# A state loop whose side work is handed out by whole uses of a PSUM bank, with delta's last piece in three and two buffers for the shared expert's copies

## The chip, the cores and the metric

One core of one Trainium2 chip runs the whole kernel in one launch. Five engines work from queues of their own and meet through semaphores: PE (TensorE, matmuls into PSUM; PEld are its weight loads), DVE (VectorE), ACT (ScalarE), POOL (GpSimd) and SP (SyncE, which issues most DMAs). The metric is device time in microseconds (us), the median of several runs.

## The reference, cut to what matters

Input x has 64 rows of 64 tokens with 256 features; `cond_1024` has one vector of 256 for each row. Four residual blocks follow. The change lies in the third (a selective state space layer, "mamba", after a recurrent layer) and in the shared expert of the fourth (a mixture of experts):

```python
x = x + L0_attn(L0_cond(x, cond))
x = x + L0_ffn(L0_cond2(x, cond))
x = x + L1_attn(L1_cond(x, cond))          # recurrent layer, then mamba
x = x + L1_ffn(L1_cond2(x, cond))          # mixture of experts, then SwiGLU experts

# L1_attn (mamba): d_inner 512, n 16
xi, z = split(x @ W_in)
xc = silu(conv4(xi) + b_conv)
delta_lr, B, C = split(xc @ W_xproj)
delta = softplus(delta_lr @ W_dt + b_dt)
dA = exp(delta[..., None] * A)
dBx = delta[..., None] * B[:, :, None, :] * xc[..., None]
h = dA_t * h + dBx_t;  y = einsum(h, C_t) + D * x_t      # scan over time
out = (y * silu(z)) @ W_out

# L1_cond2: shared experts beside eight routed ones (top 2)
for e in range(2):
    h = silu(x @ s_w1[e].T) * (x @ s_w3[e].T)
    shared_out += h @ s_w2[e].T
```

## The kernel before

**Chunks and steps.** `mamba` cuts the 4096 tokens into eight chunks of 512 (`NCH`, `CH`). With features on partitions, d_inner makes four tiles of 128 (`NI`), taken in pairs (`PI` = 2), and n is 16 states (`S`). One step of the state loop handles one pair and one state: 2 x 16 = 32 steps (`STEPS`) to a chunk and 256 in all.

**What a step does.** DVE runs two scans over time (L1094, one for each tile of the pair) in place in `hb` and multiplies both by C, broadcast over the partitions as `cb` (L1096). PE transposes the product with an identity matmul into PSUM, where the 16 states are summed (`yp`, L1109: eight matmuls). For later steps, POOL makes dx times B (`hb`, L1046, two steps ahead in the program), SP fetches B from DRAM spread over the partitions (`Bn`, L993), ACT makes dA = exp(delta * A) for the next step (L1053, two of them), and PE makes the next `cb` by a matmul with one column picked (L998). `dA` lies in PSUM in three buffers, `cb` in one, `hb` in SBUF in five.

**Side work.** Beside the steps, generators yield the rest in small pieces, from three sources:
- `urgent`: `finish` (transposes y back, L1006; adds D * x on DVE, L1008; multiplies by the gate on POOL, L1009), and after a chunk's last step `project` (the output matmuls, L1023, and the residual's add on DVE, L1026).
- `pieces`: of the next chunk, `head` (input matmuls L919 and the convolution on DVE, L926; Silu L930; the matmul L934 for delta, B and C; delta by pairs, L950 to L973), and of this chunk, `gates` (matmuls L982, copies L985, Silu L988).
- `others`: of the chunk before, `Mixture.beside`: router scores (L1499), choosing and sending rows to the experts (`send`), and the shared expert (`shared`: matmuls L1820, copies L1824 and L1827, Silu L1831, POOL's product L1828, the second matmul L1836 and its copy L1840).

A piece that leaves a sum open in PSUM yields `MID`. All of `urgent` and `pieces` use one PSUM bank, `mp`, with one buffer; all of `others` use one bank, `mq`. `turn` (L1072) hands out a piece of `urgent`, or of `pieces` where `urgent` has none; after a `MID` from either it asks `pieces`. The loop calls `turn` so that `LEFT` = 40 pieces are handed out in a chunk: 31 of `pieces` and nine of `urgent`. `islice` at j = 0 lets the head run up to the end of the first pair's delta before the second pair's gates. `BESIDE` = 56 pieces of `others` are handed out in a chunk beside that (`BESIDE_LAST` = 72 in the last).

**Delta.** Softplus is put together from functions: Relu and Abs (L959, L960), Exp (L962), two Identities (L963, L964), a subtraction (L967), Ln (L969), then an add, a subtraction and the product with xc (L970 to L972). The last four were one piece. The arithmetic is on DVE in the first chunk and on POOL in the others.

**Shared expert.** `shared` works through a chunk in two halves of 256 tokens. In each half four results of the matmul with `s3` and the rows of the output pass through an SBUF tile "up", of which the pool `work` has one buffer. `send` keeps its input in a tile "xr" of the same pool.

**What sets the order.** A scheduler takes the program's order as priority and, with estimates of its own of when things are ready, fixes each engine's queue; each engine then works its queue in order. `tc.stamp_issue_order_token` holds scans and multiplies in the program's order.

Of the kernel before, what the change touches and what calls it, by code (L numbers as in the profile page):

```python
# [13 lines left out]
F32 = mybir.dt.float32  # L14
# [7 lines left out]
P = 128  # L22
B, L, D = 64, 64, 256
NT = B * L
CH = 512
NCH = NT // CH
KD = D // P
# [830 lines left out]
MID, END = "mid", "end"  # L858


def mamba(g, w, hs, beside):
# [3 lines left out]
    nc, tc = g.nc, g.tc  # L865
    NI, S, R = w.NI, w.S, w.R
# [3 lines left out]
    NB = 2  # L870
    PI = 2
    STEPS = NI // PI * S
    LEFT = 40
    BESIDE = 56
    BESIDE_LAST = 72
    hs2 = hs.rearrange("p k b t -> p k (b t)")
# [1 line left out]
    with (  # L878
# [17 lines left out]
        rows = 2 * 32 + S  # L896
# [12 lines left out]
        def head(c, v):  # L909

            tok = ts(c, CH)
            v.xc = p2.tile([P, NI, CH], F32, name="xc")
            v.delta, v.dx, v.sz, v.ready = [], [], [], 0
            v.dbc = p1.tile([W, CH], F32, name="dbc")
            v.parts = parts[c % 2]
            for i in range(NI):
                ps = one()
                for k in range(KD):
                    nc.tensor.matmul(ps, w.Win[:, k, ts(i, P)], hs2[:, k, tok], start=(k == 0), stop=(k == KD - 1))  # L919
                    if k == 0:  # L920
                        yield MID
                acc = v.xc[:, i, :]
                nc.scalar.activation(acc, ps, AF.Identity, bias=w.col[:, 0, i : i + 1], scale=w.taps[:, i, 3:4])
                for s in range(1, 4):
                    to = seq(acc)[:, :, s:]
                    nc.vector.scalar_tensor_tensor(  # L926
                        to, seq(ps)[:, :, : L - s], w.taps[:, i, 3 - s : 4 - s], to, ALU.mult, ALU.add
                    )
                yield
            nc.scalar.activation(v.xc, v.xc, AF.Silu)  # L930
            yield
            ps = one()
            for i in range(NI):
                nc.tensor.matmul(ps[:W, :], w.Wxp[:, i, :], v.xc[:, i, :], start=(i == 0), stop=(i == NI - 1))  # L934
                if i < NI - 1:
                    yield MID
            nc.scalar.copy(v.dbc, ps[:W, :])

            v.B = tc.dram_tile((S, CH), F32, name=f"B{c}")
            nc.sync.dma_start(v.B, v.dbc[R : R + S, :])  # L940


            r = slice(C0, W)
            nc.scalar.copy(v.parts[32 : 32 + S, :], ps[r, :])
            nc.vector.tensor_sub(ps[r, :], ps[r, :], v.parts[32 : 32 + S, :])
            nc.scalar.copy(v.parts[0:S, :], ps[r, :])
            nc.vector.tensor_sub(v.parts[64 : 64 + S, :], ps[r, :], v.parts[0:S, :])
            yield


            for i0 in range(0, NI, PI):
                z, u = (p3.tile([P, PI, CH], F32, name=n) for n in ("delta", "dx"))
                v.delta.append(z)
                v.dx.append(u)
                t2, t3 = (p1.tile([P, PI, CH], F32, name=n) for n in ("t2", "t3"))
                for i in range(PI):
                    ps = one()
                    nc.tensor.matmul(ps, w.Wdt[:, ts(i0 + i, P)], v.dbc[:R, :], start=True, stop=True)
                    nc.scalar.activation(z[:, i, :], ps, AF.Relu, bias=w.col[:, 1, i0 + i : i0 + i + 1])  # L959
                    nc.scalar.activation(u[:, i, :], ps, AF.Abs, bias=w.col[:, 1, i0 + i : i0 + i + 1])  # L960
                    yield
                nc.scalar.activation(u, u, AF.Exp, scale=-1.0)  # L962
                nc.scalar.activation(t2, u, AF.Identity, bias=unit[:, 0:1])  # L963
                nc.scalar.activation(t3, t2, AF.Identity, bias=unit[:, 1:2])  # L964
                yield
                e = nc.gpsimd if c else nc.vector
                e.tensor_sub(u, t3, u)  # L967
                yield
                nc.scalar.activation(t2, t2, AF.Ln)  # L969
                e.tensor_add(z, z, t2)  # L970
                e.tensor_sub(z, z, u)
                e.tensor_mul(u, z, v.xc[:, i0 : i0 + PI, :])  # L972
                v.ready += PI  # L973
                yield
# [94 lines left out]
        urgent, pieces, others = iter(()), iter(()), iter(())  # L1069
        mid = None  # L1070

        def turn():  # L1072

            nonlocal mid
            got = next(pieces, None) if mid else next(urgent, END)
            if got is END:
                got = next(pieces, None)
            mid = got

        for s in range(LAST):  # L1080
            c, j = divmod(s, STEPS)
            p, n = divmod(j, S)
            now = vs[c]
            if j == 0:
                ahead = head(c + 1, vs[c + 1]) if c + 1 < NCH else iter(())
                pieces = chain(pieces, gates(c, now, 0), islice(ahead, 3 * NI + PI + 4), gates(c, now, PI), ahead)
                left = 0
            if n == 0:
                yp = [pp.tile([P, CH // P, P], F32, name=f"yp{i}") for i in range(PI)]
            hb, dA = hbs.pop(s), decays.pop(s)  # L1090

            for i in range(PI):
                h = hb[:, i, :]
                ins = nc.vector.tensor_tensor_scan(h, dA[i].rearrange("p b l -> p (b l)"), h, 0.0, ALU.mult, ALU.add)  # L1094
                tc.stamp_issue_order_token(ins.ins, "state")
            ins = nc.vector.tensor_tensor(hb, hb, cb.unsqueeze(1).to_broadcast([P, PI, CH]), ALU.mult)  # L1096
            tc.stamp_issue_order_token(ins.ins, "state")
            if s + AHEAD < LAST:
                ca, ja = divmod(s + AHEAD, STEPS)
                while vs[ca].ready <= ja // S * PI:  # L1100
                    turn()
                inputs(s + AHEAD)
            if s + 1 < LAST:
                decay(s + 1)
                cb = spread_c(vs[(s + 1) // STEPS], (s + 1) % S)

            for i in range(PI):
                for t in range(CH // P):
                    nc.tensor.matmul(  # L1109
                        yp[i][:, t, :],  # L1110
                        hb[:, i, ts(t, P)],
                        g.ident,
                        start=(n == 0 and t == 0),
                        stop=(n == S - 1 and t == CH // P - 1),
                        is_transpose=True,
                        skip_group_check=True,
                    )
            if n == S - 1:
                yT = [p1.tile([P, CH // P, P], F32, name=f"yT{i}") for i in range(PI)]
                for i in range(PI):  # L1120
                    nc.scalar.copy(yT[i], yp[i])
                urgent = chain(urgent, finish(c, now, p * PI, yT))
                if j == STEPS - 1:
                    urgent = chain(urgent, project(c, now))
            while left < (j + 1) * LEFT // STEPS:
                left += 1
                turn()
            most = BESIDE if c + 1 < NCH else BESIDE_LAST
            for _ in range((j + 1) * most // STEPS - j * most // STEPS):
                next(others, None)  # L1130
# [578 lines left out]
class Mixture:  # L1709
# [97 lines left out]
    def shared(self, c, x, work):  # L1807

        g, nc = self.g, self.g.nc
        NS = self.s1.shape[2] // P  # L1810
        UT = CH // 2
        for u in range(2):
            xu = x[:, :, ts(u, UT)]
            h = work.tile([P, NS, UT], F32, name="sh")
            for w in (self.s1, self.s3):
                for i in range(NS):
                    if i % 2 == 0:
                        ps = bank(g, (P, 2, UT))
                    for k in range(KD):
                        nc.tensor.matmul(ps[:, i % 2, :], w[:, k, ts(i, P)], xu[:, k, :], start=(k == 0), stop=(k == KD - 1))  # L1820
                    if i % 2:
                        to = h[:, i - 1 : i + 1, :]
                        if w is self.s1:
                            nc.scalar.copy(to, ps)  # L1824
                        else:
                            up = work.tile([P, 2, UT], F32, name="up")
                            nc.scalar.copy(up, ps)  # L1827
                            nc.gpsimd.tensor_mul(to, to, up)  # L1828
                    yield
                if w is self.s1:  # L1830
                    nc.scalar.activation(h, h, AF.Silu)  # L1831
                    yield
            ps = bank(g, (P, 2, D))
            for t in range(2):
                for i in range(NS):
                    nc.tensor.matmul(ps[:, t, :], h[:, i, ts(t, P)], self.s2[:, i, :], start=(i == 0), stop=(i == NS - 1))  # L1836
                    if i % 2 and (t, i) != (1, NS - 1):
                        yield
            rows = work.tile([P, 2, D], F32, name="up")
            nc.scalar.mul(rows, ps, 0.125)  # L1840
            to = self.made[c * CH + u * UT : c * CH + (u + 1) * UT, :]
            nc.sync.dma_start(to.rearrange("(t p) d -> p t d", p=P), rows)
# [346 lines left out]
```

## Time and profile before

The profile is of one execution. Its own time stands beside the runs':

| what | us |
|---|---|
| median of 3 runs | 2806.84 (2806.24 to 2814.49) |
| profiled execution | 2807.03 |
| its span, from the first to the last instruction | 2804.6 |
| DVE busy in the span | 1770.7 (63%) |
| PE busy | 2339.3 (83%) |
| ACT busy | 1375.5 (49%) |
| POOL busy | 1340.5 (48%) |
| first to last scan of the state loop | 698.5 to 1845.7 |

In the profile, a row of a group gives the line, the engine, the operation, what it writes and reads, the count, then busy time and mean length, and the engine's idle time before it with what ended it. "A <- B" in the waits means that A could start only when B had ended. A wait for several things is put down to the one that came last.

### The profile page before, as it was taken

The numbers are of one execution on the slowest core, as the hardware profiler recorded it, in microseconds if no ns is written. First come the engines' busy times: TensorE is split into PE (matmuls) and PEld (weight loads), VectorE is DVE, ScalarE is ACT, GpSimd is POOL, SyncE is SP. The second block draws the span as 40 slices with busy tenths as digits, with TensorE's granted clock in tenths as the row PEclk, the third lists the DMA queues.
The fourth block names the chain that finished last, engine by engine and source line by source line (L and its number), as shares of the span: only waits on it lengthen the run. The fifth ranks groups of instructions, "written<-read, shape, count | busy, mean of one in ns | idle before, by whom it ended". The sixth has DMA issues, their size and how long they took to land.

```text
span 2804.6 us, 34388 instructions
## 1 busy us (share of the span) xinstructions
PE 2339.3 (83%) x11977; PEld 1674.0 (60%) x11996; DVE 1770.7 (63%) x2980; ACT 1375.5 (49%) x2289; POOL 1340.5 (48%) x1166
## 2 busy tenths in 40 slices
PE   3989967996568888887978888687786989999995
PEld 3634436773345555554655555566664768888884
DVE  0477748973999898888889797852353442322333
ACT  0567528885466757584757676533232222222220
POOL 0022345521696868685878787835555331111110
PEclk9979988997769999998999999899998999999997
DMA  9999820002112122221121222325685755555655
GB/s 224 372 358 347 276 70 1 1 1 90 68 68 83 65 74 70 72 72 57 65 92 67 83 81 75 106 70 178 212 287 194 278 216 206 214 192 197 227 192 189
DMA packets 180501, 406.03 MB, mean 145 GB/s; under 512 B 24785, under 2 KB 84434, under 8 KB 174946
## 3 DMA queue, kind: packets, MB, share of 16 engines
q1 hardware_dynamic: 166882, 366.80, 38.4%
q0 software_dynamic: 13440, 36.98, 3.4%
q8 instruction: 96, 1.57, 0.2%
q14 instruction: 83, 0.68, 0.1%
HBM read 280.76 MB, written 144.98 MB: 152 GB/s over the span
## 4 chain that ended last, share of the span: by engine, by line
PE 43%; DVE 21%; ACT 13%; issue 9%; POOL 5%; another core or an unknown queue 2%; DMA 1%; DVEq 0%; SPq 0%; ACTq 0%; POOLq 0%
DVE hb L1094 12%; PE ps L1684 11%; PE acc L1582 8%; PE out L450 4%; DVE hb L1096 3%; ACT dA L1053 2%; PE ps L1651 2%; PE yp L1109 2%; PE mq L1820 1%; DVE xc L926 1%; PE s L416 1%; PE acc L441 1%; ACT L1053 1%; PE mp L982 1%
## 5 line engine op out<-in xcount | busy, mean ns | idle before, releaser
L1046 POOL TENSOR_TENSOR hb<-dx,Bn 128x1024 f32<-128x1024 f32 x256 | 606.4, 2377 | 269.0 <-PE yp L1109 219.7
L1094 DVE TENSOR_TENSOR_SCAN hb<-dA,hb 128x512 f32<-128x512 f32 x512 | 602.1, 1210 | 63.2 <-ACT dA L1053 59.8
L1053 ACT ACTIVATE dA<-delta,negA 128x504 f32<-128x504 f32 x512 | 345.6, 685 | 303.5 <-DVE hb L1094 298.3
L1109 PEld LDWEIGHTS yp<-ident,hb 128*128 128x128 f32 x2048 | 264.4, 150 | 160.2 <-issue 121.2
L1096 DVE TENSOR_TENSOR hb<-hb,cb 128x1024 f32<-128x1024 f32 x256 | 312.4, 1220 | 66.3 <-PE cb L998 48.0
L1684 PE MATMUL ps<-gxT,w 128*128 128x256 f32 (+1 forms) x1600 | 324.5, 361 | 1.2 <-DVE gxT L1559 0.8
L1684 PEld LDWEIGHTS ps<-gxT,w 128*128 128x128 f32 x1600 | 276.3, 190 | 47.2 <-issue 12.4
L1820 PE MATMUL mq<-x,moe_s 128*128 128x256 f32 x896 | 244.5, 405 | 66.1 <-ACT up L1827 29.9
L1109 PE MATMUL yp<-ident,hb 128*128 128x128 f32 x2048 | 298.6, 290 | 0.0
L1358 POOL DMA_INDIRECT ffn_y<-gy,to x72 | 69.2, 962 | 432.3 <-ACT gy L1584 419.8
L1820 PEld LDWEIGHTS mq<-x,moe_s 128*128 128x128 f32 x896 | 166.6, 200 | 131.7 <-ACT sh L1824 42.5
L1688 DVE TENSOR_TENSOR gh<-gs,ps 128x256 f32<-128x256 f32 (+1 forms) x200 | 78.6, 394 | 213.5 <-ACT gs L1687 206.2
L1582 PE MATMUL acc<-w,gh 128*128 128x256 f32 (+1 forms) x864 | 190.0, 390 | 0.0
L1584 ACT ACTIVATE gy<-acc,wt 128x256 f32<-128x256 f32 x152 | 67.4, 474 | 246.8 <-PE acc L1582 227.5
L1687 ACT ACTIVATE gs<-ps 128x256 f32<-128x256 f32 (+1 forms) x200 | 72.4, 364 | 235.4 <-PE ps L1684 219.3
L998 PE MATMUL cb<-parts,pick 80*128 80x512 bf16 x256 | 104.5, 408 | 88.2 <-DVE hb L1096 83.9
L1582 PEld LDWEIGHTS acc<-w,gh 128*128 128x128 f32 (+1 forms) x864 | 146.8, 191 | 30.4 <-issue 13.2
L432 POOL TENSOR_TENSOR E<-E,z 128x1024 f32<-128x1024 f32 x32 | 61.6, 1925 | 194.5 <-DVE z L431 118.0
L1358 POOL DMA_INDIRECT moe_y<-gy,to x80 | 78.0, 975 | 110.2 <-ACT gy L1584 91.3
L1582 PE MATMUL acc<-w,rh 128*128 128x256 f32 x320 | 88.5, 419 | 45.6 <-ACT rh L1653 40.3
L1572 DVE TENSOR_REDUCE wt<-pick 128x2 f32<-128x4 f32 (+1 forms) x88 | 13.6, 156 | 174.7 <-ACT gy L1584 164.0
L450 PE MATMUL out<-oT,hs 128*128 128x512 f32 x256 | 117.8, 604 | 1.5 <-ACT oT L443 1.5
(470 smaller groups left out, 4457.1 us busy)
## 6 DMA issues: line engine op xcount, KB each, us to landing
w<-ffn_w SPq DMA_DIRECT2D x40, 2176.0 KB
Bn<-B SPq DMA_DIRECT2D x128, 512.0 KB
moe_x<-fill SPq DMA_DIRECT2D x130, 260.0 KB
ffn_x<-fill SPq DMA_DIRECT2D x129, 260.0 KB
w<-moe_w SPq DMA_DIRECT2D x48, 512.0 KB
ffn_w<-in_ffn_W_dram SPq DMA_DIRECT2D x16, 640.0 KB
gx<-moe_x SPq DMA_DIRECT2D x32, 260.0 KB
gx<-ffn_x SPq DMA_DIRECT2D x32, 260.0 KB
```

The source lines that it names most:

```text
L450: nc.tensor.matmul(ps, M[:, o, ts(k, P)], v.o[:, o], start=(o == 0), stop=(o == H // 2 - 1))
L998: nc.tensor.matmul(t, pick[:, n : n + 1].to_broadcast([rows, P]), v.parts, start=True, stop=True)
L1046: nc.gpsimd.tensor_mul(hb, vs[c].dx[p], Bn[:, n % NB, :].unsqueeze(1).to_broadcast([P, PI, CH]))
L1053: nc.scalar.activation(decays[s][i][:, :, 1:], seq(vs[c].delta[p][:, i, :])[:, :, 1:], AF.Exp, scale=A[:, p * PI + i, n : n + 1],)
L1094: ins = nc.vector.tensor_tensor_scan(h, dA[i].rearrange("p b l -> p (b l)"), h, 0.0, ALU.mult, ALU.add)
L1096: ins = nc.vector.tensor_tensor(hb, hb, cb.unsqueeze(1).to_broadcast([P, PI, CH]), ALU.mult)
L1109: nc.tensor.matmul(yp[i][:, t, :], hb[:, i, ts(t, P)], g.ident, start=(n == 0 and t == 0), stop=(n == S - 1 and t == CH // P - 1), is_tran ...
L1358: i = self.g.nc.gpsimd.indirect_dma_start(out=self.y, out_offset=bass.IndirectOffsetOnAxis(ap=to, axis=0), in_=y, in_offset=None)
L1582: nc.tensor.matmul(po[s], h, w, start=(i == 0), stop=(i == n - 1))
L1684: nc.tensor.matmul(ps[:, j, :], v.w12[:, k, ts(j * (full + 1) + i, P)], v.xT[:, k, :], start=(k == 0), stop=(k == KD - 1))
L1688: nc.vector.tensor_mul(v.h[:, i, : v.rows], s, ps[:, 1, :])
L1820: nc.tensor.matmul(ps[:, i % 2, :], w[:, k, ts(i, P)], xu[:, k, :], start=(k == 0), stop=(k == KD - 1))
```

## The change

`turn` keeps the source from which it took a piece that ended in `MID` and asks the same source again until a piece ends without it; so the uses of `mp` are handed out whole. Delta's last piece is split into three: Ln, the add, and the other two. Each group so has two pieces more; `LEFT` becomes 44, and the `islice` one group longer by two. The choice of engine `e` moves up some lines. In `shared` the copies of a half and its rows go in turn to the tile "xr" (of which they use a part) and to "up", beginning with "xr".

```diff
@@ -870,7 +870,7 @@
     NB = 2
     PI = 2
     STEPS = NI // PI * S
-    LEFT = 40
+    LEFT = 44
     BESIDE = 56
     BESIDE_LAST = 72
     hs2 = hs.rearrange("p k b t -> p k (b t)")
@@ -959,15 +959,17 @@
                     nc.scalar.activation(z[:, i, :], ps, AF.Relu, bias=w.col[:, 1, i0 + i : i0 + i + 1])
                     nc.scalar.activation(u[:, i, :], ps, AF.Abs, bias=w.col[:, 1, i0 + i : i0 + i + 1])
                     yield
+                e = nc.gpsimd if c else nc.vector
                 nc.scalar.activation(u, u, AF.Exp, scale=-1.0)
                 nc.scalar.activation(t2, u, AF.Identity, bias=unit[:, 0:1])
                 nc.scalar.activation(t3, t2, AF.Identity, bias=unit[:, 1:2])
                 yield
-                e = nc.gpsimd if c else nc.vector
                 e.tensor_sub(u, t3, u)
                 yield
                 nc.scalar.activation(t2, t2, AF.Ln)
+                yield
                 e.tensor_add(z, z, t2)
+                yield
                 e.tensor_sub(z, z, u)
                 e.tensor_mul(u, z, v.xc[:, i0 : i0 + PI, :])
                 v.ready += PI
@@ -1072,10 +1074,14 @@
         def turn():
 
             nonlocal mid
-            got = next(pieces, None) if mid else next(urgent, END)
-            if got is END:
-                got = next(pieces, None)
-            mid = got
+            if mid is None:
+                mid = urgent
+            got = next(mid, END)
+            if got is END and mid is urgent:
+                mid = pieces
+                got = next(mid, END)
+            if got is not MID:
+                mid = None
 
         for s in range(LAST):
             c, j = divmod(s, STEPS)
@@ -1083,7 +1089,7 @@
             now = vs[c]
             if j == 0:
                 ahead = head(c + 1, vs[c + 1]) if c + 1 < NCH else iter(())
-                pieces = chain(pieces, gates(c, now, 0), islice(ahead, 3 * NI + PI + 4), gates(c, now, PI), ahead)
+                pieces = chain(pieces, gates(c, now, 0), islice(ahead, 3 * NI + PI + 6), gates(c, now, PI), ahead)
                 left = 0
             if n == 0:
                 yp = [pp.tile([P, CH // P, P], F32, name=f"yp{i}") for i in range(PI)]
@@ -1809,6 +1815,15 @@
         g, nc = self.g, self.g.nc
         NS = self.s1.shape[2] // P
         UT = CH // 2
+
+        def spare():
+
+            if next(names) == "up":
+                return work.tile([P, 2, UT], F32, name="up")
+            t = work.tile([P, KD, CH], F32, name="xr").rearrange("p k t -> p (k t)")
+            return t[:, : 2 * UT].rearrange("p (a t) -> p a t", a=2)
+
+        names = cycle(("xr", "up"))
         for u in range(2):
             xu = x[:, :, ts(u, UT)]
             h = work.tile([P, NS, UT], F32, name="sh")
@@ -1823,7 +1838,7 @@
                         if w is self.s1:
                             nc.scalar.copy(to, ps)
                         else:
-                            up = work.tile([P, 2, UT], F32, name="up")
+                            up = spare()
                             nc.scalar.copy(up, ps)
                             nc.gpsimd.tensor_mul(to, to, up)
                     yield
@@ -1836,7 +1851,7 @@
                     nc.tensor.matmul(ps[:, t, :], h[:, i, ts(t, P)], self.s2[:, i, :], start=(i == 0), stop=(i == NS - 1))
                     if i % 2 and (t, i) != (1, NS - 1):
                         yield
-            rows = work.tile([P, 2, D], F32, name="up")
+            rows = spare()
             nc.scalar.mul(rows, ps, 0.125)
             to = self.made[c * CH + u * UT : c * CH + (u + 1) * UT, :]
             nc.sync.dma_start(to.rearrange("(t p) d -> p t d", p=P), rows)
```

## The prediction

> **What bounds the kernel now.** I read the sums by stage first. The state loop with its lead-in is the middle row; the columns are length, busy time and count of PE, PEld, DVE, ACT and POOL, clock, DMA share and GB/s.
>
> ```profile
> 0.00:690.00 690.00, 563.20 (x3556) 354.09 (x3576) 412.26 (x603) 403.98 (x750) 201.01 (x408) 0.92 0.54 177
> 690.00:1866.00 1176.00, 945.09 (x4336) 634.76 (x4335) 1021.27 (x1005) 747.19 (x1015) 879.27 (x468) 0.91 0.21 72
> 1866.00:2804.60 938.60, 830.98 (x4089) 685.18 (x4087) 337.13 (x1372) 224.34 (x525) 260.26 (x290) 0.94 0.60 212
> ```
>
> DVE is the fullest engine there: 1021 of 1176 us. Each of 256 steps needs two scans and one multiply, 1.21 + 1.21 + 1.22 = 3.64 us, 932 us in all, and the change removes no DVE work. It can only shorten DVE's idle time. DVE's waits between 700 and 1846 us say for whom it idles (total, times, longest):
>
> ```profile
> DVE hb L1094 <- ACT dA L1053: 59.8, 38, 7.6
> DVE hb L1096 <- PE cb L998: 48.0, 34, 4.9
> DVE hb L1094 <- POOL hb L1046: 3.1, 1, 3.1
> DVE mp L945 <- ACT parts L944: 2.3, 1, 2.3
> ```
>
> So about 113 us can be won or added to. I call the chunks c0 to c7 and their 32 steps j0 to j31, counted by scans in the timeline. The largest wait for PE (4.85 us) is c3 j5; the timeline shows what PE did (start, length, engine, what, idle before):
>
> ```profile
> 1132.30 1.03 PE L1836 MATMUL mq<-moe_s,sh 128*128 128x256 f32 x4
> 1132.91 2.33 DVE L1094 TENSOR_TENSOR_SCAN hb<-dA,hb 128x512 f32<-128x512 f32 x2
> 1135.16 0.66 DVE L1026 TENSOR_TENSOR x<-x,mp 128x512 f32<-128x512 f32 x1
> 1135.87 2.99 PE L982 MATMUL mp<-hs,Win 128*128 128x512 f32 x4 [2.55 <-DVE x L1026]
> 1138.66 1.75 PE L1836 MATMUL mq<-moe_s,sh 128*128 128x256 f32 x4
> 1140.25 0.38 PE L998 MATMUL cb<-parts,pick 80*128 80x512 bf16 x1
> 1140.67 1.22 DVE L1096 TENSOR_TENSOR hb<-hb,cb 128x1024 f32<-128x1024 f32 x1 [4.85 <-PE cb L998]
> ```
>
> The gate matmul (L982) wants bank mp, which the projection's add (L1026) frees; that add stands on DVE behind two scans, and the broadcast cb that the multiply needs stands on PE behind L982 and four L1836. The old hand-out produces this: after MID from the projection, the next piece comes from the other stream, which wants the same bank.
>
> **Whole uses of a bank.** The changed order (both programs' queues were compared) finishes the projection's two uses before any gate matmul. In c1 to c4 the second add then has a multiply between it and the next cb: one L984 of 1.1 us and two scores of 1.0 us fit, by the rows, into the 3.6 us until cb is wanted. So the waits of this kind in c2, c3 and c4 go: 4.85 + 4.85 + 3.16 = **-12.9 us**. In c5, c6 and c7 they do not. There the new queue at j3 reads projection x2, shared x2, projection x2, shared x2, cb, and the second pair, the start of the second use, waits for the first use's add, which is again queued behind the next step's scans. That is the shape of the 3.16 us row of c5 today; c5, c6 and c7 lose 3.16, 4.1 and 4.0 us now and get about 3.2 each: 0 to -2, taken as **-1**.
>
> New on PE: the four L934 matmuls no longer stand in three steps but together. 4 x 1.28 us (x4 records took 2.54) after the step's transposes, plus 1.04 for these and 0.4 for cb, overrun the 6.1 us between one multiply's end and the next-but-one's start by 1.3 in c1 to c3. At j6 and j8 a shared matmul waits for copies that ACT makes behind dA (and at j8 behind a table load and a Silu): 0.5 and 1.2 over by the same sum. 3 chunks x 3.0 = 9.0, against 2 x (0.83 + 1.1) of small waits in c2 and c3 that leave: **+5**. Small waits of this sort can't all be read from a queue; today about 16 of the 48 us are of them. I add **+5**; ends -3 and +16, should a second set arise.
>
> **Delta's last piece as three, LEFT 44, islice +6.** No arithmetic is added; 16 groups get two more yields, and 35 instead of 31 pieces (44 with the urgent 9) are given out per chunk. What moves is ACT's order. A step gives ACT 3.64 us, its two dA take 1.37, and with three dA buffers dA of step s may begin only when step s-2's last scan ended. So more than about 5 us between two dA makes DVE wait. Today c2 j30 has load 1.28, Silu 1.06, copy 0.58, delta 0.68, Silu 1.91, dx 0.68, copy 0.58, load 1.28 = 8.1 us there; adding up in queue order gives a wait of 3.3, and the trace has 3.0. The next burst (Ln between two loads and a copy, 4.2 us, at j0) gives 2.4; the trace has 2.36. In the changed order Ln stands at j31 without a wait, but Silu of shared (with loads 4.5 us) at j27 meets two copies, load, Silu, delta, dx, copy, load = 6.7 us at j28: a wait of 4.9. Added over all steps, c1 to c7, such bursts make 66 us today and 60 then. Today's 66 is really 54 (59.8 less one DMA wait of 5.8, below), so I scale by 0.8: **-5**. Per chunk: c1 +0.6, c2 and c3 -1.3 each, c4 -2.3, c5 +3.1, c6 +1.1, c7 -4.8, where the shared Silu leaves j0.
>
> Here a rule speaks against the change. The Trainium skill, "ScalarE: Activation LUTs", section "Table sets: the hidden batching unit", says to batch activations by table set and not to go back and forth. ACT's queue holds 92 table loads in the loop before and 104 after, because Silu, Ln and Exp are mixed more finely. By this trace's row (1283 ns each) the 12 are 15.4 us of ACT time; by the page's price of about 2.66 us for a switch, load plus drain, 32 us. In the trace dA starts 10 ns after its load ends, so the row decides. ACT is 64% busy here, so I charge only loads that lie in a burst; they are in the 60.
>
> POOL: the add and the subtract now follow at separate turns, its work stays 4 x 2.36 us a group, and POOL runs two to three steps ahead. Its one wait of 3.1 us (c1 j30): **-2**, ends 0 and -3. In chunk 7 the rows of a second send waited 6.7 us for the first's indirect writes and DVE 5.8 us for ACT behind it. In the new queue the eight writes start some four steps earlier and DVE's table work (about 14 us) covers the second eight: **-4**. If that cover fails, eight writes at 1.27 us (0.96 and 0.3 between) before hb make POOL late by 5: ends -5 and +3.
>
> **Two buffers for the shared expert.** What ACT waits for here is little: POOL's L1828 held "up" for 3.2 us in the whole loop, ACT's idle time, not DVE's. Directly it is worth 0. But the copies can be queued earlier, which shows at the loop's end:
>
> ```profile
> 1857.13 0.86 PE mq L1820 x4
> 1857.99 3.62 PE mp L1023 x8
> 1861.61 6.92 PE mq L1836 x32
> 1868.61 0.61 ACT up L1840
> ```
>
> These 32 records are 16 matmuls, 0.43 us each. Behind the last transposes PE has 24 shared matmuls before and 12 after: 12 x 0.43 = 5.2, and a 1.9 us Silu with its load falls before the last scan: **-6**, ends -3 and -9. In return "xr" is now shared with the sends, so a load of xr waits for the previous copy's product and for the write of rows from xr. In the loop only c5 to c7 send; the loads' new places on SP are behind no Bn that is due. After the loop xr loads and shared uses of xr alternate, and the trace has no row for this wait. Queues there are nearly the same, the chain runs over PE and the sends' POOL writes: 0, ends -3 and +6.
>
> **Sum.** -12.9 - 1 + 5 + 5 - 5 - 2 - 4 - 6 = -21, rounded to -20 on the profiled execution's own 2807.0 us (span 2804.6 and 2.4 around it). The median of the runs shown, 2806.84, is within 0.2 of that. **Forecast 2787 us**, own range 2770 to 2798.
>
> **Rivals.**
> 1. **Waits move, time stays** (chance 0.17). The -12.9 turns into waits of PE for ACT's copy, since mp still has one bank, and the end's gain is given back by the sends' xr: about 2804. For it: L982 waited for the ACT or DVE that empties mp in most chunks. Against it: c1, where the add came before the multiply in the same step, shows no such wait today. That the hand-out changes nothing belongs here too, but the queues do differ.
> 2. **ACT bursts decide** (0.21), slower. If the 12 loads all land in bursts and the early Silu at j28 costs DVE its full 4.9 us in c1 to c3 on top of what the old bursts cost: +15.4 for loads, +5 x 3 for j28, less 12.9 and 6: about 2818. For it: DVE's largest wait is already ACT, and the load count. Against it: ACT has 0.36 of its time free, and today's bursts leave their places. It decides once ACT's wait rises by over 19 us.
> 3. **Half the gain of PE more** (0.1, inside "faster"): c5 to c7 are freed too, -11 more: 2776.
>
> **Numbers.** Forecast with 3: 0.62; 1: 0.17; 2: 0.21. A measurement of this kernel tells 0.3%, 8.4 us, from no change: faster 0.62, same 0.17, slower 0.21. The range leaves out the far end of 2 and the lowest of 3: 2768 to 2814.
>
> **What would show it.** The wait of the multiply for cb at j5 is gone in c2 to c4 and stands near 3 us at j4 in c5 to c7; total for cb near 40. DVE's wait for dA falls from 59.8 to about 50, its largest at j28 (c1 to c3), near 4.9. Loads in the loop 104. From the last scan to the first router matmul 23.6 us now, 17 then. I am wrong if the wait for dA passes 75, if cb waits keep 48, or if the stretch behind the loop grows over 945 us.

## The result and the profile after

The changed kernel took 2770.22 us (median of 4 runs, 2758.15 to 2772.81) where the kernel before took 2810.19 beside it: a ratio of 0.9856, interval 0.9832 to 0.988. Timed once more on another chip (run `after_again`) the ratio was 0.9865 [0.9842, 0.9888]. The forecast was 2787, so the direction was right and the gain, 40 us by medians, twice the 20 forecast. 2770.22 lies inside the forecast's range, 2770 to 2798, by 0.2 us; 0.9856 of the 2806.84 from which the forecast started would be 2766, outside it. The execution profiled took 2768.27 us, span 2766.5.

The two stages, as shown of before (length, then busy time and count of PE, PEld, DVE, ACT and POOL, clock, DMA share, GB/s):

```profile
690.00:1834.00 1144.00, 933.81 (x4349) 628.09 (x4348) 1016.49 (x1005) 760.88 (x1027) 877.22 (x468) 0.93 0.21 74
1834.00:2766.00 932.00, 823.84 (x4075) 680.10 (x4073) 337.86 (x1372) 223.00 (x524) 259.42 (x290) 0.95 0.61 214
```

The loop's stage is 32 us shorter with 4.8 us less DVE work in it, so most of the gain is idle time of DVE that went. From the start of the first scan to the end of the last, 1147.1 became 1115.8 (-31.3); from there to the end of the kernel 958.9 became 952.2 (-6.7). DVE's waits between 700 and 1830 us (total, times, longest):

```profile
DVE hb L1100 <- ACT dA L1055: 60.7, 41, 5.4
DVE hb L1102 <- PE cb L1000: 25.1, 24, 3.2
...
DVE hb L1100 <- POOL hb L1048: 0.8, 1, 0.8
```

The wait for cb fell from 48.0 to 25.1; the wait for dA did not fall. That PE no longer waits with the gate matmuls for the projection's add, as the change meant, its own waits in the loop say, before (first row) and after:

```profile
PE mp L982 <- DVE x L1026: 21.5, 14, 2.5
...
PE mp L984 <- DVE x L1028: 3.5, 5, 1.6
```

By chunk, from the timeline (gaps of 0.3 us or more inside the loop, in the chunk in which they lie, us):

| | c0 | c1 | c2 | c3 | c4 | c5 | c6 | c7 |
|---|---|---|---|---|---|---|---|---|
| length, before | 135.5 | 136.9 | 142.6 | 143.0 | 158.0 | 140.9 | 143.3 | 146.9 |
| length, after | 132.5 | 138.6 | 138.3 | 139.0 | 149.6 | 140.4 | 146.1 | 131.3 |
| wait for cb, before | 1.0 | 0.6 | 7.2 | 7.2 | 6.9 | 8.7 | 6.0 | 8.4 |
| wait for cb, after | 1.6 | 2.3 | 2.3 | 2.3 | 0.7 | 3.2 | 4.9 | 6.6 |
| wait for dA, before | 1.8 | 5.7 | 8.0 | 8.1 | 10.4 | 5.2 | 10.1 | 10.2 |
| wait for dA, after | 0.0 | 8.8 | 8.0 | 8.8 | 11.2 | 9.3 | 13.3 | 0.4 |

Half of the loop's gain is in chunk 7 (-15.6). The larger part of it are waits (9.8 for dA and 1.8 for cb), but they don't explain it all: DVE was busy there for 125.5 us before and for 120.7 after. The timeline of c7 before shows what those 4.8 us were (start, length, engine, line, what it writes and reads):

```profile
1783.32 0.96 POOL L1343 DMA_INDIRECT moe_x<-rows,moe_row  x1 [0.31 <-issue]
...
1783.66 5.38 DVE L1389 TENSOR_TENSOR i<-i,inside 128x64 f32<-128x64 f32 x1
...
1784.31 4.65 POOL L1046 TENSOR_TENSOR hb<-dx,Bn 128x1024 f32<-128x1024 f32 x2
```

A product of 128 x 64 in the table of the experts' tiles takes 5.38 us, where the others on this line take 0.2 to 0.3. I call such an operation held. It starts 0.65 us before POOL's two hb, beside the last indirect write, and ends at 1789.04, 0.1 us after POOL's second hb. Scans and multiplies run beside POOL's hb in every step and keep their 1.2 us; they take dA or cb from PSUM, this product takes everything from SBUF. The profile counts the time as busy, so no view of waits shows it. In the changed kernel:

```profile
1745.20 0.18 DVE L1403 CAST moe_tiles<-tilesf 128x48 int32<-128x48 f32 x1
...
1745.33 0.96 POOL L1349 DMA_INDIRECT moe_x<-rows,moe_row  x1 [0.30 <-issue]
...
1746.31 9.31 POOL L1048 TENSOR_TENSOR hb<-dx,Bn 128x1024 f32<-128x1024 f32 x4
```

L1403 is the table's last operation. It starts 1.1 us before POOL begins to catch up with hb, and takes 0.18 us.

At the end of the loop the chain of waits now reads (start, length, what):

```profile
1822.93 3.43 PE mp L1025 x8
1826.37 0.86 PE mq L1851 x4
1827.23 3.62 PE mp L1025 x8
1830.85 1.31 PE mq L1851 x6
1832.19 0.04 issue
1832.24 0.61 ACT up L1855
```

Between the last output matmuls and the rows' copy PE makes 6 records of L1851 in 1.31 us where it made 32 in 6.92. The router's first matmul starts 18.6 us after the last scan, 23.6 before. Both are the turn's: that matmul stands at 18.6 us in every run with the new turn, the one with a single buffer (a_nospare) included, and at 23.5 or 23.6 in every run with the old one, the one with two buffers (b_spare) included.

### The profile page after: what moved, and what is told of

Read it like the earlier page. It is cut to its first block, busy times and chain, and to the rows that moved or that the text cites. A ratio compares the mean times of both kernels' runs of the same rounds, so it can differ in the third digit from the quotient of the medians.

```text
span 2766.5 us, 34415 instructions
## 1 busy us (share of the span) xinstructions
PE 2320.8 (84%) x11977; PEld 1662.4 (60%) x11996; DVE 1766.7 (64%) x2980; ACT 1387.4 (50%) x2300; POOL 1338.1 (48%) x1166
## 4 chain that ended last, share of the span: by engine, by line
PE 45%; DVE 23%; ACT 12%; issue 9%; POOL 3%; another core or an unknown queue 2%; DMA 1%; SPq 0%; DVEq 0%; ACTq 0%; POOLq 0%
DVE hb L1100 13%; PE ps L1690 11%; PE acc L1588 9%; PE out L450 4%; DVE hb L1102 4%; PE ps L1657 2%; PE yp L1115 2%; ACT dA L1055 2%; PE mq L1835 2%; DVE xc L926 1%; PE s L416 1%; PE acc L441 1%; ACT L1055 1%; PE ps L1698 1%
## 5 line engine op out<-in xcount | busy, mean ns | idle before, releaser
L1100 DVE TENSOR_TENSOR_SCAN hb<-dA,hb 128x512 f32<-128x512 f32 x512 | 602.1, 1208 | 62.0 <-ACT dA L1055 60.7
L1102 DVE TENSOR_TENSOR hb<-hb,cb 128x1024 f32<-128x1024 f32 x256 | 311.9, 1219 | 44.1 <-PE cb L1000 25.1
L1693 ACT ACTIVATE gs<-ps 128x256 f32<-128x256 f32 (+1 forms) x200 | 72.2, 363 | 233.7 <-PE ps L1690 220.7
```

## The experiments

Each ratio is to the kernel before, run on the same chip beside it. The other columns are those of one profiled execution, in us: "c7" is the length of chunk 7, "behind" the stretch from the last scan to the end, "held" the longest held operation of the table in c7.

| run | what it is | ratio [interval] | first to last scan | c7 | behind | wait for dA | wait for cb | held |
|---|---|---|---|---|---|---|---|---|
| before | | 1 | 1147.1 | 146.9 | 958.9 | 59.8 | 48.0 | 5.38 |
| b_turn | before, new turn | 0.9991 [0.9983, 1.0] | 1148.5 | 142.5 | 953.3 | 66.6 | 34.9 | 7.17 |
| b_delta | before, split, LEFT 44, islice | 1.0074 [1.0053, 1.0095] | 1176.3 | 147.7 | 959.0 | 68.9 | 45.8 | 5.71 |
| b_spare | before, two buffers | 0.9973 [0.9959, 0.9987] | 1148.6 | 148.8 | 952.8 | 59.7 | 48.9 | 5.37 |
| a_noturn | after, old turn | 1.0066 [1.0052, 1.0079] | 1170.4 | 146.2 | 961.1 | 72.2 | 45.6 | 4.68 |
| a_nodelta | after, no split, LEFT 40 | 0.9957 [0.9942, 0.9972] | 1138.4 | 139.0 | 952.6 | 60.8 | 29.0 | 7.35 |
| a_nosplit | after, no split, LEFT 44 | 0.9876 [0.9859, 0.9893] | 1123.5 | 129.4 | 953.5 | 63.3 | 25.7 | none |
| a_nospare | after, one buffer | 0.993 [0.9912, 0.9948] | 1131.6 | 131.1 | 958.3 | 74.0 | 26.5 | none |
| after | the change | 0.9856 [0.9832, 0.988] | 1115.8 | 131.3 | 952.2 | 60.7 | 25.1 | none |
| c_slice8 | after, islice +8 | 0.9811 [0.979, 0.9833] | 1103.4 | 130.2 | 947.2 | 37.3 | 35.7 | none |
| c_slice9 | after, islice +9 | 0.9888 [0.9869, 0.9907] | 1122.6 | 129.6 | 945.2 | 36.3 | 52.6 | none |
| c_beside54 | after, BESIDE 54 | 0.9954 [0.9938, 0.9969] | 1142.7 | 144.7 | 948.7 | 69.5 | 31.3 | 7.58 |
| c_s9b52 | islice +9, BESIDE 52 | 0.9891 [0.9873, 0.991] | 1126.8 | 145.6 | 937.6 | 44.8 | 42.7 | 5.13 |

### One part alone

**The turn alone (b_turn).**

```diff
-            got = next(pieces, None) if mid else next(urgent, END)
-            if got is END:
-                got = next(pieces, None)
-            mid = got
+            if mid is None:
+                mid = urgent
+            got = next(mid, END)
+            if got is END and mid is urgent:
+                mid = pieces
+                got = next(mid, END)
+            if got is not MID:
+                mid = None
```

> The kernel before with the new `turn` alone (whole uses of mp). Theory A (the turn makes most of the 37 us): the wait for cb falls from 48.0 to about 25 as in the changed kernel, the stretch from first to last scan from 1147 to about 1127, the time by 20 us to about 2790. Theory B (the parts work only together, since the place of a piece depends on LEFT and on delta's yields): cb falls to 35 to 45, the time by under 8 us. The stretch behind the last scan stays at 959 by both.

The time moved by 0.09%, and the interval reaches to 1.0, no change. Theory A fell and B held: cb fell to 34.9, just under B's figures, but 10.4 us of new waits of L1026's add for its own matmuls and 6.8 more for dA took the loop's share back:

```profile
DVE hb L1098 <- ACT dA L1053: 66.6, 38, 7.6
DVE hb L1100 <- PE cb L998: 34.9, 34, 3.2
DVE x L1026 <- PE mp L1023: 10.4, 6, 3.6
```

At LEFT 40 the projection's matmuls stand two by two in j1 to j4, PE waits 12.2 us with them for POOL's product with the gate (1.1 before), and DVE reaches the add in its queue before the last two are done. The turn itself does what it was meant to: L982's waits for the add fall from 21.5 to 3.4. The stretch behind the loop did not stay at 959: it is 5.6 us shorter, and 5.0 of these are the router's earlier start.

**The split alone (b_delta).**

```diff
-    LEFT = 40
+    LEFT = 44
...
                 nc.scalar.activation(t2, t2, AF.Ln)
+                yield
                 e.tensor_add(z, z, t2)
+                yield
...
-islice(ahead, 3 * NI + PI + 4)
+islice(ahead, 3 * NI + PI + 6)
```

> The kernel before with delta's last piece in three, LEFT 44 and the longer islice alone. Theory A: by the prediction's term -5, so 2800 to 2806; the wait for dA falls from 59.8 to about 55, cb stays near 48. Theory B: the finer pieces do what the turn seemed to do: cb falls under 35 and the time by 15 us or more. Theory C (table loads cost): 12 more loads of 1.28 us add up to 15 us, all in the wait for dA.

It is slower by 0.74%, and all three theories missed. The loop has 101 table loads for 93 before (the one under way at the first scan counted), and is 29.2 us longer: by the timeline 9 of these are waits for dA, 9 waits for ACT's copies of B and C (L945), 9 waits of L1010 (D * x) for PE, and 4 busy time of DVE. The longest wait for dA is in c2. There ACT's timeline has Relu, Abs, a copy, Exp, a table load, the shared Silu, two Identities, a copy and another load between two dA at j29: 11.6 us from 1099.42 to 1110.98, and DVE waits 10.3 us:

```profile
DVE hb L1096 <- ACT dA L1055: 68.9, 27, 10.3
DVE hb L1098 <- PE cb L1000: 45.8, 34, 5.7
DVE xc L1010 <- PE mp L1008: 14.0, 9, 3.1
DVE mp L945 <- ACT parts L944: 11.3, 5, 4.0
```

**Two buffers alone (b_spare).**

```diff
-                            up = work.tile([P, 2, UT], F32, name="up")
+                            up = spare()
...
-            rows = work.tile([P, 2, D], F32, name="up")
+            rows = spare()
```

> The kernel before with two buffers for the shared expert's copies alone. Theory A: nothing within the loop (1147 +- 3), -6 behind the last scan (959 to 953), the time -6. Theory B: the copies' earlier places in the queues also shorten the loop: first to last scan under 1135, time -18 or more. If the end's -6 needs the turn too, the time is that of before within 3 us.

Theory A held: the loop as before (1148.6), -6.1 behind it, and 0.27% less time. But the router's first matmul stands where it stood, so these 6 us lie behind it and not where the prediction had seen them.

### One part taken away

**The old turn in the changed kernel (a_noturn; the diff of b_turn reversed).**

> The changed kernel with the old `turn`, the rest as changed. Theory A: it gives back what the turn brings, 20 us: about 2790, the wait for cb near 45 again. Theory B (parts work only together): it gives back nearly everything, over 30 us, to 2800 or more. Rival: the turn is worth little beside the finer pieces: under 2778.

It gives back everything and 18 us more. B held: the pieces' sizes and the turn go together. Its waits are near those of b_delta, and the gate matmuls wait for the projection's add again (21.6 us).

**No split, and no faster hand-out (a_nodelta; the diff of b_delta reversed).**

> The changed kernel without delta's split (LEFT 40, islice +4 as before): the new turn and the two buffers alone. Theory A (the turn frees the multiply, and delta's finer pieces with the faster hand-out make the turn's new places fit): like the new turn alone, loop 1148 +- 4, wait for dA near 66, L1026's add waiting 8 to 12 us for PE, behind the loop 950 +- 4 at best; the time 2795 to 2806. Rival B (turn and two buffers are what makes the 37 us, the split is idle): 2775 or less.

The ratio puts it 12 us below before, between the two theories and just under A's figures. L1026's add waits 12.2 us, about as A said. The loop is 10 us shorter than b_turn's, from which it differs by the two buffers alone: there ACT waits 14.3 us for POOL to release "up", here no such wait shows.

**The faster hand-out without the split (a_nosplit).**

```diff
                 nc.scalar.activation(t2, t2, AF.Ln)
-                yield
                 e.tensor_add(z, z, t2)
-                yield
...
-islice(ahead, 3 * NI + PI + 6)
+islice(ahead, 3 * NI + PI + 4)
```

> The changed kernel with Ln, add, subtraction and product as one piece again, but LEFT 44 (islice +4). Tells pace from split. If the faster hand-out is what the new turn needed: loop under 1125, time under 2778. If the split is: loop 1140 or more, time over 2795. By ACT's queue alone, adding up the pieces between two dA, the wait for dA is 73 where the same sum gives 61 for the changed kernel and 69 for turn and buffers at LEFT 40, so +12 on the changed kernel from ACT.

The pace is what the turn needed. From a_nodelta to here only LEFT goes from 40 to 44: 0.9957 to 0.9876, some 23 us of 2805. L1026's waits fall from 12.2 to 1.9; the count (j + 1) * LEFT // 32 now gives two turns at j2 instead of j3. The loop is 14.9 us shorter, and 9.6 of these are c7's: its table operation is held for 7.35 us in a_nodelta and not at all here. The forecast from ACT's queue missed: it had the wait for dA at 73 where the same sum has 61 for the changed kernel, and the trace has 63.3 where it has 60.7 there.

```profile
1758.31 7.35 DVE L1401 CAST moe_tiles<-tilesf 128x48 int32<-128x48 f32 x1
...
1758.66 6.94 POOL L1046 TENSOR_TENSOR hb<-dx,Bn 128x1024 f32<-128x1024 f32 x3
```

This is a_nodelta: the same cast that takes 0.18 us in the changed kernel ends at 1765.66, 0.06 after the third hb. Beside the changed kernel, a_nodelta's c7 is 7.7 us longer, with the same idle time of DVE (10.4 and 10.7) and 8.0 us more busy time. There the held operation makes nearly all of the difference. The split itself, with the longer islice, is worth only 0.1 to 0.2%, inside the intervals.

**One buffer in the changed kernel (a_nospare; the diff of b_spare reversed).**

> The changed kernel with one buffer "up" as before: the new turn and delta's split alone. Theory A: the loop is as in the changed kernel (1116 +- 5), behind the loop 953 as the turn alone already has it, the time 2766 to 2778. Rival B (the two buffers are needed in the loop, since the copies stand at other places): loop over 1130, the time over 2785.

Rival B held: the two buffers, worth nothing in the loop by themselves, are worth 15.8 us of it beside the other parts (and 10 beside the turn alone, by a_nodelta and b_turn). The first two lines of ACT's waits in a_nospare:

```profile
ACT dA L1055 <- DVE hb L1100: 272.1, 259, 5.9
ACT up L1833 <- POOL sh L1834: 15.8, 11, 2.7
```

ACT's timeline in a_nospare, at j28 of c2:

```profile
1087.88 0.68 ACT L960 ACTIVATE dx<-mp,mcol 128x512 f32<-128x512 f32 x1
1091.26 0.59 ACT L1833 COPY up<-mq 128x512 f32<-128x512 f32 x1 [2.70 <-POOL sh L1834]
1091.87 1.28 ACT L1055 ACT_TABLE_LOAD   x1
1093.16 0.68 ACT L1055 ACTIVATE dA<-delta,negA 128x504 f32<-128x504 f32 x1
```

In the new order the copies through "up" stand a step or less apart, inside the burst at j28. The second can't start before POOL's product has read the first; that product stands behind three hb of 2.3 us on POOL's queue; and dA stands behind the copy on ACT's. DVE waits 7.3 us there. In the changed kernel, where it waits 5.37, the same place reads:

```profile
1087.49 0.68 ACT L960 ACTIVATE dx<-mp,mcol 128x512 f32<-128x512 f32 x1
1088.92 0.59 ACT L1842 COPY xr<-mq 128x512 f32<-128x512 f32 x1 [0.75 <-PE mq L1835]
1089.53 1.28 ACT L1055 ACT_TABLE_LOAD   x1
1090.82 0.69 ACT L1055 ACTIVATE dA<-delta,negA 128x504 f32<-128x504 f32 x1
...
1091.61 1.22 DVE L1100 TENSOR_TENSOR_SCAN hb<-dA,hb 128x512 f32<-128x512 f32 x1 [5.37 <-ACT dA L1055]
```

### Moving ACT's burst

These test the sum over ACT's queue that the prediction used: the pieces between two dA, in queue order, by their rows' durations, not scaled.

**The slice longer by two (c_slice8).**

```diff
-islice(ahead, 3 * NI + PI + 6)
+islice(ahead, 3 * NI + PI + 8)
```

> The changed kernel with islice longer by two (3 * NI + PI + 8): delta's Relu and Abs of the second group go ahead of the second pair's gates, at j25 and j26 instead of j28. By the sum over ACT's queue the burst at j28 in c1 to c3 (4.9) becomes 2.3 + 2.4 and the total wait for dA falls from 61 to 50, in c4, c5 and c6 most. If ACT's bursts are DVE's waits as the sum has them: loop 1105 +- 5, time 2755 to 2765. If what goes there comes back as waits for PE or POOL: time within 5 of 2770.

The sum ranked it rightly (50 against 61; measured 37.3 against 60.7), with the same 104 table loads in the loop. PE took part of it back:

```profile
DVE hb L1100 <- ACT dA L1055: 37.3, 31, 3.5
DVE hb L1102 <- PE cb L1000: 35.7, 28, 4.0
```

The loop is 12.4 us shorter than the changed kernel's, as the first theory had it, and the kernel is faster: 0.9811 [0.979, 0.9833] of before, against 0.9865 [0.9842, 0.9888] when the changed kernel was timed again:

> The changed kernel as it is, timed in more rounds, so that it can be set beside the slice longer by two (0.9811 of before, interval 0.979 to 0.9833). If that version is really faster, this one stands at 0.985 to 0.989; if the two are alike, at 0.980 to 0.984.

It came to 0.9865, in the first of the two bands; these intervals don't meet. That of the first measurement (0.9832 to 0.988) just touches that of c_slice8.

**The slice longer by three (c_slice9).** The same edit with 9.

> The changed kernel with islice longer by three (3 * NI + PI + 9): Exp and the two Identities of the second group also go ahead of the second pair's gates. By the sum over ACT's queue the total wait for dA is 45 (50 with the slice longer by two, which the chip gave as 37), but it has a burst of 5.7 at j26 in c1 to c3. If that sum ranks kernels: 2745 to 2753. If the sum is too coarse for 4 us, or PE's waits (35.7 with the slice longer by two) grow further: 2753 to 2765.

A miss for the sum: the wait for dA stays (36.3), but cb's grows to 52.6, as the second theory had it, though the time (2767.9) is above its band, and the whole is no faster than the changed kernel. A sum over ACT's queue alone says nothing of PE's.

**BESIDE 54 (c_beside54).**

> The changed kernel with BESIDE 54 instead of 56: nothing else differs but where the shared expert's pieces fall. The sum over ACT's queue gives a wait for dA of 71 instead of 61 with the same 104 table loads. If ACT's bursts set the loop: time 2778 to 2785. If the place of these pieces doesn't matter: 2765 to 2775.

Slower than forecast: 0.9954, near 2792 where before is 2805. The wait for dA came as the sum had it (69.5 for 71). But 13 us of the loop's 27 are c7, where a product of the table was held for 7.58 us beside three hb.

**Slice +9 and BESIDE 52 (c_s9b52).**

> The slice longer by three with BESIDE 52. The sum over ACT's queue gives 43.5, the lowest of those worked out; but what is left of the shared expert at a chunk's end is then handed out at one go at j3, on PE ahead of cb. If ACT decides: 2742 to 2752. If PE's part takes it back: over 2758, with waits for cb of 45 or more.

The second theory held in the time (2768.81) and nearly in the wait for cb (42.7); dA came as summed (44.8 for 43.5). c7 is back at 145.6 with two operations held, 3.09 and 5.13 us. The stretch behind the loop, 937.6, is the shortest of the table. No version here beats c_slice8.

## Why the prediction was right, point by point

**Whole uses, -12.9.** Right in place and about right in size. The waits for cb in c2, c3 and c4 fell from 21.3 to 5.3 in sum, -16.0, and the cause is the one named: the gate matmuls' wait for L1026's add is 1.6 to 3.5 us in the runs with the new turn and 18.4 to 21.6 in those with the old one. But the turn alone does not shorten the kernel: at LEFT 40 the gain is exchanged for waits of L1026's add itself, for dA, and for cb in c1. Its time is rival 1's (2804 forecast, 2805.4 measured), though only half by rival 1's way: waits did move, but the end's gain, which rival 1 saw lost, stayed. The pace of 44 kept the gain in the loop; the prediction had charged LEFT with nothing but ACT's order.

**c5 to c7, -1.** The shape was right: one wait of 3.16 us stands in each. The size was off: the chunks' waits for cb fell by 8.4 in sum, since the smaller ones of c5 (1.85, 1.63 and 1.30 us) went as well.

**New waits of PE, +5, and small waits, +5.** Both mis-sized. Of the three waits forecast for each of c1 to c3, two came: what stands in the queues at j6 and j8 holds up the multiplies of j7 and j9. In c2:

```profile
1000.87 1.22 DVE L1102 TENSOR_TENSOR hb<-hb,cb 128x1024 f32<-128x1024 f32 x1 [1.24 <-PE cb L1000]
...
1009.09 1.22 DVE L1102 TENSOR_TENSOR hb<-hb,cb 128x1024 f32<-128x1024 f32 x1 [1.07 <-PE cb L1000]
```

They were forecast at 0.5 and 1.2. The four L934 together bring no wait of 0.3 us or more. So c1 to c3 have 6.9 us of such waits for the 9.0 forecast, and 5.3 of small ones left for 3.9: some +2 for the +5. The other +5, the addition for what can't be read, was not needed: c0 has 0.6 more, and c4's small waits fell by 3.0. With -12.9, -1, +5 and +5 the prediction had -3.9 for cb; measured is -22.9.

**ACT's order, -5.** The step that failed. In c1 to c6 the wait for dA rose by 11.9 us, where the prediction had about zero. The bursts stand where it put them (4.5 to 5.4 us at j28 in c1 to c3, forecast 4.9). The sum for the changed kernel was right too: 60 against 59.8 in c1 to c7. What failed is the sum for the order before, 66 where 54 were measured. The prediction took the excess for a common factor of 0.8 and scaled the difference of the two sums by it, and there is no such factor: the same sum is 8 to 13 us too high for a_nodelta (69 for 60.8), a_nosplit (73 for 63.3), c_slice8 (50 for 37.3) and c_slice9 (45 for 36.3), and right within 2 for the changed kernel, c_beside54 and c_s9b52. Why it is too high for some orders is open. Set against what was measured before, the sum said +6.

**The loads.** The rule that speaks against going back and forth between table sets did not decide. 104 loads are in the loop of the changed kernel, of b_turn and of c_slice8, which stand at 60.7, 66.6 and 37.3 us of waiting for dA; b_delta has 101 and is the slowest. The timelines shown point to what else lies between the same two dA. Rival 2's time, slower, came in b_delta and a_noturn (by 21 and 18 us), but only in part by its way: the wait for dA rose by 9.1 and 12.4 us, where rival 2 asks for over 19, and b_delta lost as much again at L945 and at L1010.

**POOL, -2.** Right (3.1 to 0.8).

**Chunk 7's sends, -4.** Right mechanism, wrong size; with the Silu's -4.8 that leaves j0, the prediction had some -9, and c7 lost 15.6. The writes start 36 us into the chunk instead of 56, four steps earlier as forecast; the wait of 5.8 us for ACT is gone, and the table's work does cover the second eight. What it did not see is the 5.4 us product in the profile before, because it took all of DVE's busy time as work ("the change removes no DVE work"). By the table above, c7 takes 139 to 149 us in every kernel with a held operation and 129 to 131 in every one without. The held operation is nearly all of that difference in a_nodelta, and about a third of it in the kernel before, where the rest is waits. The table was not moved by itself.

**Two buffers, directly 0.** True in the order before (b_spare) and wrong in the new one: -15.8 (a_nospare to after). The prediction read the hold of "up" from the trace before, 3.2 us, and did not ask what it would be in the order that it had just worked out. Its -6 for the end came out right in size (-6.7) by luck. The fewer matmuls ahead of the router, from which it was worked out, are the turn's (5.0 us in every run with it, none in b_spare). Behind the router's first matmul the buffers went with 6 us less in b_spare (against before) and in the changed kernel (against a_nospare), but not in a_nodelta (against b_turn, 0.7) nor in a_noturn (against b_delta, 2.2 more). What that stretch follows is open: each of these is one execution, and the times of the changed kernel itself spread over 15 us.

**The sum.** In the loop the prediction had -15: -3.9 for cb, -9 for dA (ACT's order and chunk 7) and -2 for POOL. Measured are -31.3: -22.9 for cb, +0.9 for dA, -2.3 for POOL, -4.8 of DVE's busy time, which it had at nothing, and some 2 of smaller waits. So the direction was right for the reason named, the turn's, but that the time lies in the range is luck: cb won 19 us more than forecast, and dA 10 less. Of its signs, the place of the waits for cb and of the bursts came, the total for cb (25 for 40) and for dA (60.7 for 50) did not, and none of the three by which it would have been wrong did (the stretch behind the loop, 938.6 in the prediction's row, is 932.0).

## What to carry to other kernels

A wait for a buffer is read from the order in which the work will stand, not from today's trace: the second buffer was worth nothing in the old order and 16 us in the new one. Parts of a hand-written schedule don't add up: alone the turn took 0.1% off (an interval that reaches to none), the buffers 0.3%, and the split with its pace put 0.7% on, yet all together took 1.4% off; judge the order as a whole, and look for the engine's heaviest stretch between two instructions that the bound engine waits for. An instruction far longer than its own kind can hide a wait that no list of waits has.

## What the runs showed of the hardware

**DVE held by POOL.** In c7 a small DVE operation with its operands in SBUF can end only when POOL's run of hb has ended: 5.38 us beside two hb, 7.17, 7.35 and 7.58 beside three, each ending 0.1 us or less after the last; alone the same operations take 0.2 to 0.3. In c4 products of 128 x 128 are held in the same way beside a single hb, in the changed kernel too (1.33, 1.78 and 1.98 us). The Trainium skill, "SBUF — State Buffer", section "SBUF: two separate sides", says that DVE and GpSimd share one pair of SBUF ports by an exclusive lock: whichever starts first, GpSimd or a DVE operation with two SBUF inputs or in a mode that uses both ports, holds it for its whole instruction, while the other waits. The runs agree that one waits, and add that the loser may lose several times in a row: it gets no turn between one hb and the next. Who starts first does not fit: by their rows seven of the nine operations held in c7 start 0.2 to 0.7 us before the first hb, beside POOL's last indirect write, though beside the writes before it the table's operations keep their 0.2 to 0.3 us. Why they don't end in time is open. Casts and operations with a scalar, with one SBUF input, were held like products with two (7.17 and 5.37 us).

**One chip is faster behind the loop, not in it.** `after_again` ran on a chip where the kernel before takes 2758 us. The loop is 1115.8 us in both profiles of the changed kernel; the stretch behind it is 906.5 instead of 952.2.
